# A two-layer graph network on one core: one segment sum as a 64-column matmul, another message order, and a rearranged prologue

## The chip, the core and the metric

The kernel runs on one core of a Trainium2 chip. The core has engines with queues of their own: TensorE (PE, with PEld for its weight loads), VectorE (DVE), ScalarE (ACT), GpSimd (POOL) and SyncE (SP); transfers are issued from a queue and run on 16 DMA engines. The metric is device time in microseconds (us). Everything is fp32. Seven runs of the kernel before took 5893.01 to 5935.96 us, with a median of 5921.59.

## The reference, cut to what matters

There are 6250 nodes with 160 features (64 scalars and 32 vectors of 3 components), and 200000 edges, sorted by destination. Each of two layers does this, and then adds x and normalizes:

```python
xs, xv  = mixed node features          # 64 scalars, 32 x 3 vector components
w       = silu(e @ W_fc1) @ W_fc2      # per edge: w0 (64), w1 (64), w2 (32), w3 (32)
gs, gv  = xs[src], xv[src]             # gathered by edge
mid0a   = w0 * gs * e_s                # "A": scalars from scalars
mid0b   = w3 * sum_c(gv * e_v) / sqrt3 # "D": scalars from vectors
mid1a   = w1 * gs * e_v                # "C": vectors from scalars
mid1b   = w2 * gv * e_s                # "B": vectors from vectors
agg     = segment_sum([mid0a, mid0b, mid1a, mid1b], dst) / 4
x       = layernorm(x + C_S * self(x) + C_X * mix(agg))
```

The second layer has 96 and 128 channels in place of some of these, and a gate at its end.

## The kernel before, in words

**Edges.** The 200000 edges are cut into 1563 tiles of 128. `plan()` (L37) puts 3 to 12 consecutive tiles into each of 284 groups such that the destinations of a group should fit a window of W = 32 nodes. In the prologue the kernel checks that they do; if the flag says so (L991), it takes the fast path `windows()` (L594), first for layer 1 (i = 0), then for layer 2, and otherwise a slow general path, which does not run here.

**The loop of `windows()`** (L831) goes over 391 units of four tiles, as a software pipeline. For each unit it

- gathers the source rows of the unit four ahead (`gather`, POOL, one indirect DMA a tile, L710, eight pair buffers);
- makes the hidden layer of the unit three ahead (`hidden`: PE matmuls into `pair`, ACT Silu into `h`, L672 and L683);
- makes the edge weights of the unit two ahead (`weights`: 192 columns a tile into a `pw` bank), the selectors `sel` (`places`, DVE, L741: for each tile four blocks of 32 columns, one each for e_s, e_x, e_y, e_z, with the edge attribute where the destination matches) and the messages `mid` (`products`, DVE, L728: four instructions for two tiles in layer 1);
- turns the sums of groups that ended in the unit before (`turn`, L775: PE transposes of `r` into the upper half of a `pair` bank, L143, then two DVE adds into `sm` and `sr`, L788 and L790, at a column offset loaded from `base`);
- sums its own four tiles (`aggregate`, L751);
- does one or two steps of the node blocks (`prepare` and `proceed`: tiles `pn`, `nx`, `xt`, `rm0`, `rr0`).

The order of PE instructions is pinned to program order (L138 and L143, the helpers `matmul` and `transpose`), so on PE a late operand holds up all that follows. Since all matmuls go through L138, its groups in a profile are told apart by their tiles and shapes.

**The sum.** In `aggregate` each selector block of a tile is a matmul of its own with 32 weight columns, at `tile_position=(0, 32 * c)`, so that the four results lie in the partitions 0, 32, 64 and 96 of one `pg` bank. Which of the 32-wide blocks of `mid` each multiplies is in `sums` (L605), as (first block, step, number):

```python
        sums = (((5, 2, 5), (0, 2, 3), (2, 1, 3), (2, 2, 3)),
                ((9, 1, 5), (2, 1, 5), (0, 2, 5), (0, 1, 5)))[i]
```

In layer 1 the selector of e_s therefore moves 160 columns and the other three 96 each. At a group's end ACT copies `pg` into `r` (L766: 128x96; L768: the other 64 columns of 32 rows).

**The prologue** (L148 to L430) takes the nodes in 13 chunks (twelve of four blocks of 128, then a tail of 106 rows). `turn_nodes` transposes a chunk on PE; the copies `xt` go to DVE and ACT in turn, and `zt` to ACT. `send_nodes` multiplies by `l1` and `l1z`, scales on ACT (L284), adds on DVE (L285) and stores to `table`. `check()` comes after the sixth chunk: two casts, a small matmul, 11 subtracts, three reduces and two subtracts on DVE, with `limits` set by POOL earlier. `checked()` makes the flag after the last chunk. Then 12 matmuls compose the weights of the node step (`w23` into a `pw` bank), and 13 small DVE copies put them into `rm0` and `rr0` (L389 to L397). The first gather on POOL (L710) comes after that.

Of the kernel before, what the change touches and what calls it, by code (L numbers as in the profile page):

```python
# [9 lines left out]
F32 = mybir.dt.float32  # L10
I32 = mybir.dt.int32
AF = mybir.ActivationFunctionType
OP = mybir.AluOpType
# [3 lines left out]
P = 128  # L17
# [69 lines left out]
def kernel(ctx: ExitStack, tc: tile.TileContext, a, out):  # L87
# [34 lines left out]
    SLOTS = (448, 640)  # L122
# [25 lines left out]
    chunks = [range(b, min(b + BG, NB - 1)) for b in range(0, NB - 1, BG)] + [range(NB - 1, NB)]  # L148
# [12 lines left out]
    def spread(t, s, v, n, q):  # L161

        nc.vector.memset(t, 0.0)
        q.dma_start(t[0:S, 0:n], a[s])
        for k in range(2):
            q.dma_start(t[S + k * V:S + k * V + V, n + k * V:n + k * V + V], a[v])
# [3 lines left out]
    spread(l1[:, 0], "Ws_l1_a", "Wv_l1_a", S, nc.scalar)  # L170
    spread(l1[:, 1], "Ws_l1_c", "Wv_l1_c", S, nc.scalar)
    ident = const.tile([P, P], F32, name="ident")
    make_identity(nc, ident)
    for j, (k, q) in enumerate((("a", nc.scalar), ("c", nc.gpsimd))):
        for r in range(0, P, V):
            q.dma_start(l1z[r:r + V, j, :], a[f"Wv_l1_{k}"])
# [47 lines left out]
    rm0 = const.tile([96, 4, 2, S + V], F32, name="rm0")  # L224
    rr0 = const.tile([64, 2, 2 * V], F32, name="rr0")
# [4 lines left out]

    limits = pre.tile([1, 2, NG], F32, name="limits")
    nc.gpsimd.memset(limits[:, 0], 0.0)
    for b, g in enumerate(READY):
        if g < NG:
            nc.gpsimd.memset(limits[:, 0, g:min(READY[b + 1], NG)], float(P * (b + 1)))
    g0 = 0
    while g0 < NG:
        g1 = g0
        while g1 < NG and zeroed(g1) == zeroed(g0):
            g1 += 1  # L240
        nc.gpsimd.memset(limits[:, 1, g0:g1], float(zeroed(g0) - W))
        g0 = g1

# [4 lines left out]
    def turn_nodes(bs, x):  # L248

        m, n = len(bs), rows_of(bs[0])  # L250
        p = psum.tile([P, 512], F32, name="pw", bufs=3)
        for j in range(m):
            transpose(p[:, j * P:j * P + n], x[:n, j, 0:P], ident[:n, :n])
        last = work.tile([P, BG * V], F32, name="xz")
        nc.vector.tensor_copy(last[:n, :m * V].rearrange("p (j d) -> p j d", d=V), x[:n, 0:m, P:D])
        z = pair[0][:, 0:P]
        transpose(z[:m * V, :n], last[:n, :m * V], ident[:n, :n])
        xt = work.tile([P, BG * P], F32, name="xt", bufs=2)
        zt = work.tile([P, P], F32, name="zt", bufs=2)
        w = (m - 1) * P + n  # L260
        if (bs[0] // BG) % 2:
            nc.scalar.activation(xt[:, :w], p[:, :w], AF.Copy)
        else:
            nc.vector.tensor_copy(xt[:, :w], p[:, :w])
        nc.scalar.activation(zt[:m * V, :n], z[:m * V, :n], AF.Copy)
        return xt, zt

    def send_nodes(bs, xt, zt):
        n = rows_of(bs[0])
        rows = work.tile([P, BG, D], F32, name="rg", bufs=2)  # L270
        qs = []
        for j in range(len(bs)):
            tag, k = (("pg", 2), ("pn", 1), ("pg", 2), (None, 0))[j]
            p = psum.tile([P, 512], F32, name=tag, bufs=k) if tag else pair[1]
            q = p[:n, :2 * D].rearrange("p (w d) -> p w d", w=2)
            matmul(q[:, :, 0:P], xt[:, j * P:j * P + n], l1, start=True, stop=True)
            qs.append(q)
        for j, q in enumerate(qs):
            v = slice(j * V, j * V + V)
            matmul(q[:, :, P:D], zt[v, :n], l1z[v], start=True, stop=True,  # L280
                   tile_position=(j * V, 0))
        for j, (b, q) in enumerate(zip(bs, qs)):
            t = rows[:n, j, :]
            nc.scalar.activation(t, q[:, 0, :], AF.Copy, scale=nv[:n, b, 0:1])  # L284
            nc.vector.scalar_tensor_tensor(t, q[:, 1, :], nv[:n, b, 1:2], t,  # L285
                                           op0=OP.mult, op1=OP.add)
        if n == P:
            nc.sync.dma_start(
                table[0][bs[0] * P:(bs[-1] + 1) * P, :].rearrange("(j p) d -> p j d", p=P),
                rows[:, :len(bs), :])  # L290
        else:
            nc.sync.dma_start(table[0][bs[0] * P:N, :], rows[:n, 0, :])
# [8 lines left out]

    def check():

        basef = pre.tile([1, NG], F32, name="basef")
        nc.vector.tensor_copy(basef, base)
        nc.vector.tensor_copy(off, raw)
        p = psum.tile([P, 512], F32, name="pw", bufs=3)
        matmul(p[:, :NG], ones, basef, start=True, stop=True)
        for g0, g1 in segments:
# [3 lines left out]
            nc.vector.tensor_tensor(o, o, p[:, g0:g1, None].to_broadcast([P, m, n]), OP.subtract)  # L313

        nc.vector.memset(off[tail_e:, NT - 1:], 0.0)
        ends = pre.tile([P, 2], F32, name="ends")
        nc.vector.tensor_reduce(ends[:, 0:1], off, AX.X, OP.max)
        nc.vector.tensor_reduce(ends[:, 1:2], off, AX.X, OP.min)

        nc.vector.tensor_scalar(ends[:, 0:1], ends[:, 0:1], float(W - 1), None, op0=OP.subtract)  # L320
        nc.vector.scalar_tensor_tensor(over, ends[:, 1:2], -1.0, ends[:, 0:1],
                                       op0=OP.mult, op1=OP.max)

        nc.vector.tensor_tensor(limits[:, 0], limits[:, 0], basef, OP.subtract)
        nc.vector.tensor_tensor(limits[:, 1], basef, limits[:, 1], OP.subtract)
        nc.vector.tensor_reduce(tops[:, 1:2], limits, AX.XY, OP.max)

    def checked():
# [7 lines left out]
    previous = None  # L336
    for c, (bs, x) in enumerate(zip(chunks, xs)):
# [4 lines left out]
        if c == 5:  # L342
            check()
    send_nodes(previous[0], *previous[1])
    checked()


# [26 lines left out]

    p = psum.tile([P, 512], F32, name="pw", bufs=3)
    q = p[:96, :192].rearrange("p (j d) -> p j d", j=2)

    for j in range(2):
        for o, w, m in ((q[:, j, 0:S], w23[:, j * 96:j * 96 + 96], w23[:, 192:256]),
                        (q[:, j, S:], w23[:, 256 + j * 96:352 + j * 96], w23[:, 448:480])):
            matmul(o, w, m, start=True, stop=True)
        for k in range(2):
            matmul(p[k * V:k * V + V, 192 + j * V:224 + j * V],
                   w23[:, 320 + j * 96:352 + j * 96], w23[:, 448:480], start=True, stop=True,
                   tile_position=(0, k * V))
    nc.vector.tensor_copy(rm0[0:64, 0, :, 0:S], q[0:64, :, 0:S])  # L389
    nc.vector.tensor_copy(rm0[64:96, 0, :, S:], q[64:96, :, S:])  # L390

    for c, at_c, at_d in ((1, (32, 64), 0), (2, (0, 64), 32), (3, (0, 32), 64)):
        for k, r in enumerate(at_c):
            nc.vector.tensor_copy(rm0[r:r + 32, c, :, S:], q[32 * k:32 * k + 32, :, S:])
        nc.vector.tensor_copy(rm0[at_d:at_d + 32, c, :, 0:S], q[64:96, :, 0:S])
    for k in range(2):
        nc.vector.tensor_copy(  # L397
            rr0[k * V:k * V + V, :, k * V:k * V + V],
            p[k * V:k * V + V, 192:256].rearrange("p (j d) -> p j d", j=2))
# [76 lines left out]
    def second_nodes(b, work, clear, name="nx"):  # L476
# [26 lines left out]
        def summed():  # L503
            p = psum.tile([P, 512], F32, name=bank[0], bufs=bank[1])
            q = p[:n, :2 * D].rearrange("p (w d) -> p w d", w=2)
            for c in range(4):
                l = sm[:96, c, rows]
# [6 lines left out]
            matmul(q[:, :, S + V:D], sr[:64, rows], rr0, start=False, stop=True)  # L514
# [79 lines left out]
    def windows(i, loads, work, inputs_of):  # L594
# [4 lines left out]
        scalar = lambda w, place: (w, V, 0, 2, place, 2)  # L599
        vector = lambda w, place, step, c=0, n=3: (w, 0, S + c * V, n, place, step)  # L600
        kinds = ((scalar(0, 2), scalar(S, 5), vector(128, 9, 2), vector(160, 0, 3)),
# [3 lines left out]
        sums = (((5, 2, 5), (0, 2, 3), (2, 1, 3), (2, 2, 3)),  # L605
                ((9, 1, 5), (2, 1, 5), (0, 2, 5), (0, 1, 5)))[i]
# [144 lines left out]
        def aggregate(t):  # L751
# [6 lines left out]
            for c, (at, step, k) in enumerate(sums):  # L758
                o = mid[:n, t % 2, V * at:V * at + V]
                o = bass.AP(tensor=o.tensor, offset=o.offset, ap=[o.ap[0], [V * step, k], [1, V]])  # L760
                matmul(pg[32 * c:32 * c + 32, :k * V], s[:n, t % 2, c, :], o,
                       start=first, stop=last, tile_position=(0, 32 * c))
            if last:
                r = work.tile([P, 160], F32, name="r")
                w = (96, P)[i]
                nc.scalar.activation(r[:, :w], pg[:, :w], AF.Copy)  # L766
                if i == 0:
                    nc.scalar.activation(r[:32, 96:], pg[:32, 96:160], AF.Copy)  # L768
# [6 lines left out]
        def turn(g):  # L775
            r = made["r", g]
            pt = pair[g % 2][:, 2 * P:]
            if i == 0:
                transpose(pt[:96, :P], r[:, :96], ident)
                transpose(pt[:64, P:P + W], r[:32, 96:160], ident[:32, :32])  # L780
            else:
                transpose(pt[:, :P], r[:, :P], ident)
                matmul(pt[:, P:P + W], rest[g % 3], fold, start=True, stop=True)
            with tc.issue_after(made["last"].ins):
                b = nc.vector.value_load(base[0:1, g:g + 1], min_val=0, max_val=NP - W)  # L785
            at = bass.ds(b, W)
            h, k = ((96, 64), (P, P))[i]
            nc.vector.tensor_tensor(  # L788
                sm[:h, :, at], pt[:h, :P].rearrange("p (c w) -> p c w", c=4), sm[:h, :, at], OP.add)
# [90 lines left out]
    def general(i, loads, work):  # L880
# [18 lines left out]
        def body(t, n):  # L899
# [51 lines left out]
            if i == 0:  # L951
                put = [a0, a1, bx, dx, c0[1], c1[1], c0[2], dy, c1[2], c0[3], c1[3], dz, by, bz]
# [25 lines left out]
        h = (96, P)[i]  # L978
        into = [(h * k, h, lambda c, k=k: sm[:h, k, c]) for k in range(4)]
        into.append((4 * h, slots - 4 * h, lambda c: sr[:slots - 4 * h, c]))  # L980
# [76 lines left out]
```

## Time and profile before

| | value |
|---|---|
| median of 7 runs | 5921.59 us (5893.01 to 5935.96) |
| the profiled execution: time, span | 5933.25 us, 5931.5 us |
| mean granted TensorE clock | 0.75 |
| busy PE / PEld / DVE / ACT / POOL | 4430.0 / 2879.7 / 3052.3 / 1172.3 / 3078.7 us |
| first gather | 65.64 us after the start |

The table is of the profiled execution but for its first line. Busy time is a union of an engine's instructions, and matmuls overlap, so a mean duration times a count is more than the busy time. The duration of a single matmul includes its way through the array: what one costs in a row of many is read from the starts. A matmul in fp32 appears as two records, its two passes. In a line "a <-b", b is what ended the idle time of a. Layer 1 lies between some 66 and 3000 us, layer 2 after it.

### The profile page before, as it was taken

To read this page: it belongs to the slowest core of one execution; us is meant where nothing else is said; L and a number is where in the kernel's file an instruction comes from. 1 tells how busy PE (TensorE), PEld (TensorE's weight loads), DVE (VectorE), ACT (ScalarE), POOL (GpSimd) and SP (SyncE) were. 2 spreads that over 40 slices of the span, in tenths; PEclk is the share of its full clock that TensorE was granted. 3 is DMA by queue.
4 is the path that set the end of the run, shared out by engine and by line. 5 is a ranking of instruction groups with operands and counts; after the bars stand their busy time and mean duration, and the time that the engine had idled before them with its cause. 6 is when DMAs were issued, how large, how long until landed. Compare 5 with 4: busy or idle time off the path is not lost. (4 is left out here: it accounts for less than half of the span.)

```text
span 5931.5 us, 108061 instructions
## 1 busy us (share of the span) xinstructions
PE 4430.0 (75%) x37363; PEld 2879.7 (49%) x37363; DVE 3052.3 (51%) x13202; ACT 1172.3 (20%) x4012; POOL 3078.7 (52%) x3232
## 2 busy tenths in 40 slices
PE   7788777777777777787866676777677776777877
PEld 4555555555555555555534444444444444444544
DVE  5554444444444454444545555555555555555555
ACT  2111111111122222222210111111112222222333
POOL 4555555555555455454445555555555555544543
PEclk7777777777777777777777777777777777777777
DMA  3222222222222222222222222222222222222221
GB/s 102 60 61 59 57 56 55 53 55 52 55 54 54 50 56 55 52 55 52 53 63 66 66 69 68 71 67 68 66 67 67 68 69 67 65 63 64 66 64 44
DMA packets 298517, 364.06 MB, mean 61 GB/s; under 512 B 86323, under 2 KB 246204, under 8 KB 297964
## 3 DMA queue, kind: packets, MB, share of 16 engines
q0 software_dynamic: 151056, 257.36, 18.0%
q1 hardware_dynamic: 121740, 85.59, 5.6%
q10 hardware_dynamic: 25168, 14.11, 0.8%
q8 instruction: 301, 4.93, 0.3%
q14 instruction: 252, 2.06, 0.1%
HBM read 338.73 MB, written 18.03 MB: 60 GB/s over the span
## 5 line engine op out<-in xcount | busy, mean ns | idle before, releaser
L710 POOL DMA_INDIRECT g<-table,src x3126 | 3056.9, 978 | 2811.3 <-DVE mid L728 1579.6
L728 DVE TENSOR_TENSOR mid<-g,pw 128x128 f32<-128x128 f32 (+2 forms) x7820 | 1840.8, 297 | 426.8 <-remote 197.2
L138 PE MATMUL pg<-mid,sel 128*32 128x160 f32 (+1 forms) x25008 | 1582.3, 353 | 245.1 <-issue 242.9
L138 PE MATMUL pw<-fc,h 100*128 100x192 f32 (+1 forms) x6252 | 1491.7, 432 | 289.4 <-issue 229.9
L138 PEld LDWEIGHTS pw<-fc,h 100*128 100x128 f32 (+1 forms) x6252 | 1051.0, 233 | 778.6 <-issue 705.8
L741 DVE SCALAR_TENSOR_TENSOR sel<-iota,off,ea 128x128 f32<-128x128 f32 x3126 | 945.8, 340 | 686.0 <-remote 412.5
L138 PEld LDWEIGHTS pg<-mid,sel 128*32 128x32 f32 x25008 | 945.4, 133 | 629.3 <-issue 489.5
L143 PE MATMUL pair<-ident,r 128*96 128x128 f32 (+1 forms) x852 | 264.2, 335 | 704.1 <-ACT h L683 314.5
L138 PE MATMUL pair<-e,fc 64*100 64x256 f32 (+1 forms) x2348 | 727.7, 524 | 75.7 <-issue 49.6
L788 DVE TENSOR_TENSOR sm<-pair,sm 96x128 f32 (+1 forms) x568 | 163.9, 289 | 1177.1 <-PE pair L143 357.6
L143 PEld LDWEIGHTS pair<-ident,r 128*96 128x96 f32 (+1 forms) x852 | 125.1, 147 | 927.5 <-ACT h L683 356.8
L766 ACT ACTIVATE r<-pg 128x96 f32<-128x96 f32 (+1 forms) x568 | 149.7, 264 | 1977.0 <-remote 866.7
L138 PEld LDWEIGHTS pair<-e,fc 64*100 64x100 f32 (+1 forms) x2348 | 300.6, 215 | 322.0 <-issue 266.7
L672 ACT ACTIVATE h<-pair 100x256 f32<-100x256 f32 x782 | 258.3, 378 | 925.3 <-remote 357.2
L683 ACT ACTIVATE h<-pair 128x256 f32<-128x256 f32 x392 | 150.3, 384 | 957.7 <-remote 380.4
L138 PE MATMUL pn<-rm,sm 96*128 96x128 f32 (+3 forms) x968 | 199.7, 353 | 50.6 <-issue 42.0
L138 PEld LDWEIGHTS pn<-rm,sm 96*128 96x128 f32 (+2 forms) x968 | 177.5, 235 | 71.8 <-issue 61.5
L772 ACT ACTIVATE rest<-pg 32x32 f32<-32x32 f32 x1136 | 209.5, 184 | 12.8 <-issue 0.3
L517 DVE SCALAR_TENSOR_TENSOR nx<-pn,gets,nx 128x160 f32<-128x160 f32 x96 | 36.5, 380 | 200.1 <-PE pw L138 71.4
L138 PEld LDWEIGHTS pair<-fold,rest 128*128 128x128 f32 x568 | 132.8, 285 | 13.5 <-ACT rest L772 8.1
L458 ACT ACT_TABLE_LOAD x95 | 121.9, 1283 | 1.9 <-DVE mv L457 0.3
L143 PE MATMUL pn<-ident,nx 128*128 128x128 f32 (+1 forms) x242 | 65.4, 362 | 74.0 <-DVE nx L460 67.9
(153 smaller groups left out, 1473.5 us busy)
## 6 DMA issues: line engine op xcount, KB each, us to landing
g<-table,src POOLq DMA_INDIRECT x3126
e<-in_e SPq DMA_DIRECT2D x781, 64.0 KB
e<-in_e SPq DMA_DIRECT2D x390, 20.0 KB
ea<-in_ea_main SPq DMA_DIRECT2D x63, 96.0 KB
xg<-in_x_main SPq DMA_DIRECT2D x12, 320.0 KB
table<-rg SPq DMA_DIRECT2D x12, 320.0 KB
xmid<-nx ACTq DMA_DIRECT2D x48, 80.0 KB
table<-nr ACTq DMA_DIRECT2D x48, 80.0 KB
```

The source lines that it names most:

```text
L138: r = nc.tensor.matmul(*args, **kw)
L143: r = nc.tensor.transpose(*args)
L458: nc.scalar.activation(mv[:n, 1:2], mv[:n, 1:2], AF.Sqrt, bias=eps[:n])
L517: nc.vector.scalar_tensor_tensor(y, q[:, k, :], gets[:n, b, k:k + 1], y, op0=OP.mult, op1=OP.add)
L672: nc.scalar.activation(h[:100, 2 * P * j:2 * P * j + m], pair[j][:100, :m], AF.Silu)
L683: nc.scalar.activation(h[:kk, c0:c1], p[:kk, c0:c1], AF.Silu, scale=0.125)
L710: nc.gpsimd.indirect_dma_start(out=g[:n, j, :], out_offset=None, in_=table[i][:, :], in_offset=bass.IndirectOffsetOnAxis(ap=of(t)[0], axis=0))
L728: nc.vector.tensor_tensor(parts(mid[:n, :m], V * place, V * step, k), parts(g[:n, :m], c, V, k), parts(q[:n, :m], w, w_step, k), OP.mult)
L741: made["last"] = nc.vector.scalar_tensor_tensor(s[:n, j], iota[:n, None, :].to_broadcast([n, 4, W]), w, e[:, :, None].to_broadcast([n, 4, ...
L766: nc.scalar.activation(r[:, :w], pg[:, :w], AF.Copy)
L772: nc.scalar.activation(rest[g % 3][k, k], pg[k, P:P + V], AF.Copy)
L788: nc.vector.tensor_tensor(sm[:h, :, at], pt[:h, :P].rearrange("p (c w) -> p c w", c=4), sm[:h, :, at], OP.add)
```

## The change

The y and z selector blocks of layer 1 become one matmul with 64 weight columns. For that both must multiply the same blocks of `mid`, so the order of messages in layer 1 becomes Dx, C0, Dy, C1, Dz, A0, A1, Bx, By, Bz. e_s takes the five last (160 columns), e_x the first four, and e_y and e_z both the blocks 1 to 4 (128 columns; what one of them doesn't need is computed too and multiplied by zero weights later, or meets its own weights in `rm0`):

```diff
-        sums = (((5, 2, 5), (0, 2, 3), (2, 1, 3), (2, 2, 3)),
-                ((9, 1, 5), (2, 1, 5), (0, 2, 5), (0, 1, 5)))[i]
+        sums = (((0, 1, 5, 1, 5), (1, 1, 0, 1, 4), (2, 2, 1, 1, 4)),
+                ((0, 1, 9, 1, 5), (1, 1, 2, 1, 5), (2, 1, 0, 2, 5), (3, 1, 0, 1, 5)))[i]
...
-            for c, (at, step, k) in enumerate(sums):
+            for c, m, at, step, k in sums:
...
-                matmul(pg[32 * c:32 * c + 32, :k * V], s[:n, t % 2, c, :], o,
+                matmul(pg[32 * c:32 * (c + m), :k * V],
+                       s[:n, t % 2, c:c + m, :].rearrange("p c w -> p (c w)"), o,
                        start=first, stop=last, tile_position=(0, 32 * c))
             if last:
                 r = work.tile([P, 160], F32, name="r")
-                w = (96, P)[i]
-                nc.scalar.activation(r[:, :w], pg[:, :w], AF.Copy)
+                nc.scalar.activation(r[:, :P], pg[:, :P], AF.Copy)
                 if i == 0:
-                    nc.scalar.activation(r[:32, 96:], pg[:32, 96:160], AF.Copy)
+                    nc.scalar.activation(r[:32, P:], pg[:32, P:P + V], AF.Copy)
```

A tile of layer 1 thus has three matmuls: 32 weight columns with 160 moved, 32 with 128, and 64 with 128, in this order. Layer 2's matmuls are those of before. What hangs on it: `sm` takes 128 rows in layer 1 (96 before) and `sr` 32 (64), the turn transposes 128 and 32 columns, `rm0` and `rr0` are laid out accordingly, and a node block has one matmul more:

```diff
-            matmul(q[:, :, S + V:D], sr[:64, rows], rr0, start=False, stop=True)
+            matmul(q[:, :, S + V:S + 2 * V], sm[:, 0, rows], rr0[:, 0], start=False, stop=False)
+            matmul(q[:, :, S + 2 * V:D], sr[:V, rows], rr0[:V, 1], start=False, stop=True)
```

The prologue is arranged anew: the tail chunk comes first; `l1` is cleared once; of the loads of `l1` and `l1z`, ACT issues the four of "a" and POOL the four of "c" (before, ACT issued ten and POOL four); the `xt` copy of the tail goes to DVE; the casts, the 11 subtracts, the clearing of `limits` and its two subtracts move to POOL; the reduces stay on DVE, one a chunk, after the last add of that chunk; the weights are composed after the eighth chunk, copied by ACT out of PSUM, and placed by DVE in steps of three a chunk; the flag is made ahead of the last `send_nodes`:

```diff
-    chunks = [range(b, min(b + BG, NB - 1)) for b in range(0, NB - 1, BG)] + [range(NB - 1, NB)]
+    chunks = [range(NB - 1, NB)] + [range(b, min(b + BG, NB - 1)) for b in range(0, NB - 1, BG)]
...
-            nc.vector.tensor_tensor(o, o, p[:, g0:g1, None].to_broadcast([P, m, n]), OP.subtract)
+            nc.gpsimd.tensor_tensor(o, o, base_of[:, g0:g1, None].to_broadcast([P, m, n]),
+                                    OP.subtract)
...
-        if c == 5:
+        if c == 3:
+            nc.gpsimd.tensor_copy(basef, base)
+            nc.gpsimd.tensor_copy(off, raw)
+        if c == 6:
+            bases()
             check()
+        if c == 7:
+            small = composed()
+        if c > 7:
+            for step in small[:3]:
+                step()
+            small = small[3:]
+        if c > 8 and reduces:
+            with tc.issue_after(last[0].ins):
+                reduces.pop(0)()
+    assert not small and not reduces
+    checked()
     send_nodes(previous[0], *previous[1])
-    checked()
```

## The prediction, before the result was known

> **What bounds the kernel now.** I read the busy shares first, then layer 1 alone (100 to 2950 us): its windows, its waits and its TensorE groups with the shapes kept apart, then timelines of single units, and last the prologue. The window of layer 1 (columns: length, then busy time and instructions of PE, PEld, DVE, ACT and POOL, granted clock, DMA share, GB/s), and what PE waited for there (total, times, longest):
>
> ```profile
> 100.00:2950.00 2850.00, 2231.56 (x18717) 1509.52 (x18709) 1379.04 (x5712) 532.38 (x1698) 1510.39 (x1539) 0.75 0.23 55
> ```
> ```profile
> PE pair L143 <- ACT h L672: 281.7, 85, 7.5
> PE pg L138 <- issue: 100.0, 179, 1.2
> PE pn L143 <- DVE nx L460: 64.6, 38, 7.3
> ```
>
> PE is busy 2232 of 2850 us; no other engine passes 1511. The 618 us of idle PE are few and long (the first line: 85 waits of 3.3 us). A layer has 391 units of four tiles, so one takes about 7.3 us, 5.7 of them PE work; POOL's four gathers take 4 x (0.98 + 0.30) = 5.1 us. So layer 1 is a PE chain with holes, at a granted clock of 0.75 (slices of 2 us show 1.00 and 0.50, with 0.50 after a hole).
>
> Next the groups that the change touches (busy, mean ns; then idle before), and two stretches of PE (start, length, instructions), the first two lines at clock 1.0, one unit at 0.5, then two tiles at each clock:
>
> ```profile
> L138 PE MATMUL pw<-fc,h 100*128 100x192 f32 x3080 | 803.7, 409 | 52.3 <-issue 49.1 <-DVE mid L728 1.1 <-PE pair L138 0.3
> L138 PE MATMUL pg<-mid,sel 128*32 128x160 f32 x3082 | 710.2, 380 | 17.1 <-issue 16.6
> L138 PE MATMUL pg<-mid,sel 128*32 128x96 f32 x9247 | 549.8, 307 | 84.1 <-issue 83.4
> ```
> ```profile
> 1015.22 1.57 PE L138 MATMUL pw<-fc,h 100*128 100x192 f32 x8
> 1016.71 1.27 PE L138 MATMUL pg<-mid,sel 128*32 128x160 f32 x32
> ```
> ```profile
> 1005.02 2.34 PE L138 MATMUL pg<-mid,sel 128*32 128x160 f32 x32
> ```
> ```profile
> 1028.98 1.28 PE L138 MATMUL pg<-mid,sel 128*32 128x160 f32 x16
> ...
> 1032.80 0.73 PE L138 MATMUL pg<-mid,sel 128*32 128x160 f32 x16
> ```
>
> A unit's sum is 4 tiles x 4 matmuls x 2 passes of fp32 = 32 records. At clock 1.0, 32 take 1.27 us and 16 take 0.73, so two tiles more cost 0.54: **0.27 us a tile**; at 0.5, (2.34 - 1.28) / 2 = **0.53 us**. The eight pw records of 192 columns take 1.57 us, and a row of five 1.08: 0.163 us each, 0.85 ns a column. Two passes of 160 columns are thus 0.27 us, while a tile's four matmuls one after another would be 2 x (160 + 3 x 96) x 0.85 = 0.76. So the four column strips run beside each other, and only the widest, 160 columns, is paid for.
>
> **The change, part by part.**
>
> *Fewer matmuls in a tile's sum.* 4 become 3, or 8 records fewer of some 98 in a unit. But the x strip keeps its 160 columns. If the 64-column matmul still runs beside the other two, a tile costs 0.27 us as before: nothing gained. The three narrow strips ended early and hid behind the wide one; at 128 columns they still do.
>
> *A second tile shape.* This is the price I expect to decide. In the trace, PE waits whenever the shape of its array tile changes. From the last pw (100 x 128) to the first pg (128 x 32), from pg to pair, and from pair to pw, the next matmul starts 93 to 97 ns after the stream before it could have ended at clock 1.0, and 134 to 138 ns at 0.5 (medians over hundreds of pairs); between matmuls of one shape it is 2 ns. The wait is also there where the tiles don't overlap: after the 32-row whoz matmuls, none of 91 pair matmuls on rows 64 to 127 starts within 200 ns, though those rows are free; after a 64-row tile on rows 0 to 63 they start 13 ns later. So two shapes don't share the array. No row shows 128 x 32 beside 128 x 64, so the cost has two ends: nothing, if these two can mix; or, if not, per tile a group of two 32-column strips (2 x 160 columns), a switch, the 64-column group (2 x 128 columns, alone), and a switch back. The Trainium skill, "TensorEngine Tiling (Array Packing)", section Tiling Modes, speaks against the change: it lists 128x64 and 128x32 as separate configurations and says "Changing tiling mode (not just tile) drains the TensorE"; it gives no duration; by it the sum takes the upper end, without it nothing.
>
> The upper end: a 64-column group is 128/160 of 0.27 or 0.53, so 0.21 or 0.43 us. Four tiles add 4 such groups and 7 switches (the first into pg and the last out of it are there now):
> clock 1.0: 4 x 0.213 + 7 x 0.095 = 1.52 us a unit; clock 0.5: 4 x 0.427 + 7 x 0.137 = 2.67 us.
> At a mean clock of 0.75 half the time, so two thirds of the work, is at 1.0: 2/3 x 1.52 + 1/3 x 2.67 = 1.90 us. Times 391: **743 us** of PE time. I take this end, since the nearest rows (switches in columns from 128 to 32, in rows between disjoint tiles) all drain.
>
> How much of it reaches the end? PE's holes can take some. The turn (L143) waits for the r copy and ACT h, 281.7 us, and node steps for DVE nx, 64.6 us: together 346, in which PE has nothing else in its fixed order; a later pg would fill them only if what it waits for does not itself come after pg. ACT's r copy does come after pg, so 346 is generous; all 618 us of idle PE is the other bound. So +743 - 346 = **+397 us**, between +125 (743 - 618) and +743. Late next would be POOL: at 5.1 of then 8.3 us a unit it is further off than now, so no cover from there.
>
> *mid in another order, r, sm and the turn.* The same four DVE products a pair, of the same sizes. r goes from 128x96 and 32x64 to 128x128 and 32x32; ACT is busy 532 of 2850 us. The first transpose has 128 weight columns for 96, with the same 128 moved. sm adds 128 rows for 96, sr 32 for 64: DVE lengths go by elements per row, which stay. One more matmul per node block: 49 x 2 passes x 64 columns x 0.85 ns = 5 us at most, halved clocks aside; taken in the range, 0 here.
>
> *Prologue.* The first gather starts at 65.64, held by the small copies into rr:
>
> ```profile
> POOL g L710 <- DVE rr L397: 39.7, 1, 39.7
> ```
> ```profile
> 7.23 1.28 ACT L265 ACT_TABLE_LOAD   x1 [7.23 <-DMA l<-in_Wv_l_c]
> ```
> ```profile
> 30.03 2.41 DVE L313 TENSOR_TENSOR off<-off,pw 128x444 f32<-128x444 f32 x11
> ...
> 33.32 1.76 DVE L317 TENSOR_REDUCE ends<-off 128x1 f32<-128x1563 f32 x1
> 35.01 1.76 DVE L318 TENSOR_REDUCE ends<-off 128x1 f32<-128x1563 f32 x1
> ...
> 37.48 0.67 DVE L264 COPY xt<-pw 128x512 f32<-128x512 f32 x1
> ```
>
> Three savings. ACT issues ten loads before its table load, about 0.5 us each (its queue rows 0.76 to 7.20); six fewer let it start about 3 us sooner, though the first x must be there too: -3 to 0. Check holds DVE from 30.03 to 37.48, and PE has a hole of 6.07 us before 38.49. The subtracts and casts (2.41 + 0.87 + 1.02 us) go to POOL, which stands idle for 39.7 us; the reduces (2 x 1.76 + 0.72) stay on DVE, spread over three chunks behind the last rg. I take 4 of the hole's 6 us. POOL's price for a subtract is not shown; from its 128x768 memset (0.76 us) to its 128x128 ident (0.33 us), 1563 columns of cast and subtract are 3 to 8 us, and with the limits' memsets (0.33 + 0.71 + 2.42) still inside the cover; without cover a late check would hold the last reduce and the first gather by what it lacks, a few us. The 13 copies into rm0 and rr0 (61.83 to 65.1, 3.3 us) are spread over chunks where DVE waits for ACT; the flag and the last send remain: -2.5. The queues: on SP the short tail of x goes first; POOL issues four l1 loads as before (others than before), ahead of its dst loads. Sum **-10 us**, from 0 to -13.
>
> **Sum.** The profiled run took 5933.25 us (span 5931.5), 12 above the median of 5921.59. 5933 + 397 - 10 = **6320 us**.
>
> **Rivals.**
>
> *A: the shapes mix.* The 64-column matmul runs beside the others. For: both use all 128 rows, and the strips run independently now. Against: every other switch seen. Then only the prologue counts: 5933 - 10 = 5923, no change to be told.
>
> *B: faster, since fewer matmuls shorten the holes.* In the trace, pg's last matmul often counts as finished 0.7 to 8 us late while three or more gathers run back to back; the turn then waits (281.7 us <-ACT h), the clock falls to 0.5, and the next unit runs at half speed. I can't explain these holes. If they come from the number of pg matmuls in flight (a quarter fewer now), they shrink: about 98 in layer 1 are over 2.5 us, 517 us in sum; a quarter is 130, so 5933 - 10 - 130 = 5793. It needs A too, or a gain above the drain's price. It decides against me from 397 us of holes closed.
>
> *C: the full price.* The added PE time makes pg, r and the turn later in every unit, no hole fills, and 0.5-clock stretches last longer: 5933 + 743 - 10 = 6666. For it: by a fit over layer 1's units, a microsecond of node matmuls goes with 2.4 (± 0.3) us more of its unit, so PE time is hardly ever hidden.
>
> *D: the holes take all.* 5933 + 125 - 10 = 6048.
>
> **Chances.** Forecast with its neighbours C and D: drain, 0.75 (forecast 0.45, C 0.17, D 0.13). A 0.12, of which 0.07 within 0.3% and 0.05 faster; B 0.13. A difference under 0.3% (18 us) can't be told from none here. So faster 0.18, same 0.07, slower 0.75. The range leaves out the ends of B and C: 5780 to 6700.
>
> **What would show it.** In layer 1, pg stretches of a unit with 24 records of 2.8 us at clock 1.0 instead of 32 of 1.27, 64-column records starting 95 ns after the 32-column stream, PE busy in the layer up by some 700 us, the ACT h wait shrunk. If pg still takes 1.27, A or B holds, and the number and length of the <-ACT h waits tells which. In the prologue, the first gather near 56. I would be wrong if two column widths share the array, or if the holes go with the matmuls' number.

## The result, and the profile after

The changed kernel takes **6005.58 us** (median of 19 runs, 5936.12 to 6056.32) against 5925.79 us for the kernel before (46 runs, 5888.35 to 5962.09): the ratio is 1.0118, with a 95% interval of 1.010 to 1.0137. It is slower, as forecast, but by 80 us between the medians (70 by the ratio) and not by the 387 of the prediction. The ratio leaves out runs over 1.5% above the fastest, the profiled execution (6030.64 us, span 6028.9) among them; its clock, 0.796, is that of the others (0.793 to 0.812).

Layer 1 in the same window as before (length, then busy time and instructions of PE, PEld, DVE, ACT and POOL, granted clock, DMA share, GB/s), and three lines of what PE waited for there:

```profile
100.00:2950.00 2850.00, 2600.92 (x15277) 1466.79 (x15275) 1338.75 (x5546) 514.05 (x1633) 1490.43 (x1501) 0.84 0.22 53
```
```profile
PE pair L143 <- ACT h L701: 168.9, 68, 6.1
PE pn L143 <- DVE nx L487: 15.6, 13, 3.4
PE pg L138 <- issue: 14.9, 33, 0.9
```

PE is busy for 2601 us of the window instead of 2232, at a granted clock of 0.84 instead of 0.75. The waits that the prediction listed are shorter: 169 us for 282, 16 for 65, and 15 for 100. The groups that the change touches:

```profile
L138 PE MATMUL pg<-mid,sel 128*32 128x160 f32 x3000 | 798.7, 353 | 4.2 <-issue 4.2
L138 PE MATMUL pg<-mid,sel 128*64 128x128 f32 x2998 | 745.3, 335 | 8.2 <-issue 7.9
L138 PE MATMUL pg<-mid,sel 128*32 128x128 f32 x3000 | 699.2, 320 | 3.1 <-issue 2.9
L138 PE MATMUL pw<-fc,h 100*128 100x192 f32 x3000 | 684.2, 378 | 3.0 <-issue 2.9
```

The 64-column matmuls are busy for 745 us. The three pg groups overlap, so this line does not yet say that they don't hide behind the others; the starts below do. The pw matmuls, which nobody changed, take 684 us instead of 804 for nearly as many: the higher clock. One unit of the changed kernel at clock 1.0:

```profile
522.16 3.08 PE L138 MATMUL pg<-mid,sel 128*32 128x160 f32 x24
525.16 0.68 PE L138 MATMUL pair<-e,fc 64*100 64x256 f32 x4
```

From the first of the 24 records to the next operation it takes 3.00 us. In the kernel before, 32 records took 1.21, from 1016.71 in the prediction's stretch to the next operation:

```profile
1017.92 0.46 PE L138 MATMUL pair<-e,fc 64*100 64x256 f32 x2
```

The medians over the whole units of layer 1 are 3.01 and 1.20 us at clock 1.0, and 5.16 and 2.27 at 0.5. Between a 32-column and a 64-column matmul, in either direction, the next starts 95 to 96 ns (at clock 1.0) after the stream before it could have ended, as at the switches of shape in the prediction (93 to 97 ns).

To see where the layer's time went, I give each moment from the first gather to the last of layer 1 either to the matmul that PE is in (of two that overlap, the later) or to idle:

| layer 1, us | pg | pw, pair, pn | idle | sum | clock |
|---|---|---|---|---|---|
| before | 726 | 1519 | 637 | 2882 | 0.750 |
| after | 1373 | 1308 | 271 | 2952 | 0.843 |
| difference | +647 | -211 | -366 | +70 | |

So 647 us were added. Idle time took 366 of them, and 211 came back because all other matmuls ran at the higher clock: if each moment of pw, pair and pn is weighted with the granted clock, they take 1131 us before and 1114 after, so their work hardly changed. The 70 us that are left are most of the 97 between the two profiled spans. The rest lies outside layer 1: layer 2, whose instructions are the same, took 2919 us for 2906, and the passage between the layers 53 for 39.

In the prologue nothing was won between these two executions. The first gather starts at 65.68 us (65.64 before):

```profile
58.80 3.65 SPq L279 DMA_DIRECT2D table<-rg  x2
```
```profile
65.68 1.05 POOL L739 DMA_INDIRECT g<-table,src  x1 [23.12 <-issue]
```

The last store of `table` is issued at 62.05 (the second of the two) and its semaphore reaches POOL at 64.53; in the kernel before it was issued at 61.52 and came at 64.33. The gather follows 1.2 to 1.3 us later in both. Single executions scatter here: over all traces of the experiments below and these two, the first gather comes at 65.6 to 67.4 us in the four executions that have the prologue of before (before, before_too, slow_before, yz_only; mean 66.6), and at 61.3 to 66.4 in the eight with the whole new one (mean 64.0). So some 2 to 3 us are won on average, of the 10 that were forecast.

### The profile page after: what moved, and what is told of

The parts are those of the page before. It is cut to its first block, busy times and chain, and to the rows that moved or that the text cites. A ratio compares the mean times of both kernels' runs of the same rounds, so it can differ in the third digit from the quotient of the medians.

```text
span 6028.9 us, 101994 instructions
## 1 busy us (share of the span) xinstructions
PE 4887.0 (81%) x34331; PEld 2876.6 (48%) x34331; DVE 3049.4 (51%) x13185; ACT 1176.2 (20%) x4015; POOL 3117.0 (52%) x3248
## 5 line engine op out<-in xcount | busy, mean ns | idle before, releaser
L138 PE MATMUL pg<-mid,sel 128*32 128x160 f32 x21882 | 2268.4, 361 | 190.4 <-issue 188.6
L138 PEld LDWEIGHTS pg<-mid,sel 128*32 128x32 f32 x21882 | 1057.6, 132 | 1203.0 <-issue 1106.3
L138 PE MATMUL pw<-fc,h 100*128 100x192 f32 (+1 forms) x6252 | 1367.0, 417 | 200.5 <-issue 148.8
L816 DVE TENSOR_TENSOR sm<-pair,sm 128x128 f32 x568 | 165.3, 291 | 1357.5 <-PE pair L143 531.6
L143 PE MATMUL pair<-ident,r 128*128 128x128 f32 x852 | 245.0, 313 | 610.9 <-ACT h L712 352.1
L795 ACT ACTIVATE r<-pg 128x128 f32<-128x128 f32 x568 | 157.2, 277 | 1945.2 <-PE pg L138 999.0
L143 PEld LDWEIGHTS pair<-ident,r 128*128 128x128 f32 x852 | 118.9, 140 | 813.7 <-ACT h L712 395.6
L138 PE MATMUL pn<-rm,sm 128*128 128x128 f32 (+3 forms) x968 | 180.1, 333 | 17.8 <-issue 17.1
L138 PEld LDWEIGHTS pn<-rm,sm 128*128 128x128 f32 (+1 forms) x968 | 161.8, 218 | 28.7 <-issue 26.4
L138 PE MATMUL pair<-fold,rest 128*128 128x32 f32 x568 | 112.1, 285 | 8.7 <-issue 5.5
```

The costliest lines, as they stand in the source:

```text
L138: r = nc.tensor.matmul(*args, **kw)
L143: r = nc.tensor.transpose(*args)
L795: nc.scalar.activation(r[:, :P], pg[:, :P], AF.Copy)
L816: nc.vector.tensor_tensor(sm[:, :, at], pt[:, :P].rearrange("p (c w) -> p c w", c=4), sm[:, :, at], OP.add)
```

## The experiments

My theory after the result: two widths of column tile don't share the array, as forecast, but what of that time is paid is what idle PE and the granted clock don't take, and the prologue is worth nothing, since the last store of `table` is the gate. The rivals: the loss comes from the rest of the layer's change (message order, 128 rows of `sm`, the matmul more in a node block), or from the prologue, or switching does harm beyond its TensorE time.

The experiments ran in five groups, each on one chip, and each is compared with the kernel before on its chip. That matters here: in four groups the kernel before takes 4097 to 4103 us instead of 5926. Only one group (tail_first, early_mix, late_check, slow_bal) met a chip like the first, with 5834.

### One part alone

Layer 1 as before, with the new prologue (`p_only`). 

> Layer 1 as before, the prologue of the change alone. Theory: the prologue is worth nothing, since the first gather waits for the last table store to land (64.33 us before, 64.53 after), so the first gather stays at 65.5 to 66 us and the ratio is 1.000 (0.998 to 1.002). Rival, the step on record: first gather near 56 us, 10 us less, ratio 0.998. Second rival: the prologue carries part of the loss, ratio 1.003 or more.

Measured: 4129.44 against 4103.35 us, ratio 1.0076 (1.0047 to 1.0106). The first gather is at 61.6 us (67.4 in the kernel before on that chip). Neither my theory nor the forecast holds: the prologue makes the kernel slower. This is taken up below.

The prologue as before, with the change in layer 1 (`yz_only`). 

> Prologue as before, the layer-1 sums and message order of the change alone. Theory: the whole loss is here, ratio 1.010 to 1.014, clock in layer 1 0.84 for 0.75, TensorE idle in layer 1 down by some 360 us. Rival (prologue carries part of it): 1.007 or less.

Measured: 4439.58 us, ratio **1.0832** (1.0808 to 1.0855), clock 0.996 in layer 1, 39 us idle. The loss is in layer 1, but it is 336 us here, nearly five times the result's. All that I had expected of its size was wrong, which made the chip itself the question.

```diff
-        sums = (((0, 1, 5, 1, 5), (1, 1, 0, 1, 4), (2, 2, 1, 1, 4)),
+        sums = (((0, 1, 5, 1, 5), (1, 1, 0, 1, 4), (2, 1, 1, 1, 4), (3, 1, 1, 1, 4)),
```

That edit makes y and z two matmuls of 32 weight columns again, with all else as changed (`split`). 

> The changed kernel with y and z as two matmuls of 32 weight columns and 128 moved each, all else as changed. Theory (the 64-column shape is the cause): a unit's sum takes 1.27 us at clock 1.0 again, layer 1's clock is back at 0.75, ratio 0.998 to 1.002. Rival (message order, 128-row sm, the matmul more in a node block): the loss stays, 1.010 to 1.014.

```profile
536.24 1.27 PE L138 MATMUL pg<-mid,sel 128*32 128x160 f32 x32
537.45 0.49 PE L138 MATMUL pn<-who,xt 128*128 128x128 f32 x2
```

Measured: 1.0058 (1.0039 to 1.0077); the unit's sum is 1.21 us again, and layer 1 takes 2027 us with 268 idle at a clock of 0.906 (the kernel before on this chip: 2016, 262 and 0.902). The loss in layer 1 is gone, so the message order, the 128-column strips and the additional node matmul cost next to nothing. What is left is that of `p_only`.

The changed kernel with a unit's 32-column matmuls ahead of its 64-column ones (`quad`):

```diff
-                for t in range(4 * u, min(4 * u + 4, NT)):
-                    if t == 4 * u + 2:
-                        prepare()
-                    aggregate(t)
...
+                for t in ts:
+                    aggregate(t, (0, 1) if i == 0 else range(4), i == 1)
+                if i == 0:
+                    if len(ts) > 2:
+                        prepare()
+                    for t in ts:
+                        aggregate(t, (2, 3))
```

> The changed kernel with all 32-column matmuls of a unit first and its four 64-column matmuls after them: one switch of shape inside a unit instead of seven, the same streams. Theory (a 64-column group runs alone and is paid in full, and switches come on top): the unit's sum at clock 1.0 takes 1.27 + 4 x 0.21 + 0.1 = 2.2 us instead of 2.8, so two thirds of the loss are left, ratio 1.006 to 1.010. Rival (only the switches cost, the 64-column streams are hidden): 1.5 us, ratio 1.000 to 1.003.

```profile
532.43 2.29 PE L138 MATMUL pg<-mid,sel 128*32 128x160 f32 x24
534.65 0.49 PE L138 MATMUL pn<-who,xt 128*128 128x128 f32 x2
```

Measured: 2.22 us from the first record to the next operation, so both the streams and the switches are paid, as the theory has it. The ratio is 1.0178 (1.0156 to 1.020), above the expected range, which was meant for the first chip: 39 us more in layer 1 than the kernel before has there, where the change costs 325.

### The chip, and what TensorE time is

The kernel before (`before_too`) and the changed one (`after_too`) once more on the chip of the first group. 

> The kernel before once more, for its profile on the chip on which the others run. Where it takes about 4100 us, theory: TensorE idle in layer 1 of 250 to 300 us instead of 635, few holes over 2.5 us, granted clock above 0.9, first gather at 65.5 to 66.5 us. Rival (the shorter time comes from faster gathers or vector work): POOL and DVE instructions are shorter than on the first chip (978 and 297 ns), clock and holes as there.

> The changed kernel once more. A unit's sum costs 3.0 us at clock 1.0 for 1.2, so 1.8 x 391 = 708 us. Theory: holes and clock pay for a part of it, so on a chip with 270 us of idle TensorE in layer 1 the rest is +300 to +400 us, ratio 1.075 to 1.095; on a chip with 635 us of idle 1.010 to 1.014 again. Rival (a loss that does not go with the chip's holes): 1.012 everywhere.

The windows of both, from 100 to 2000 us, before and then after:

```profile
100.00:2000.00 1900.00, 1649.26 (x17774) 1170.84 (x17772) 1309.95 (x5417) 504.58 (x1594) 1429.84 (x1479) 0.90 0.32 79
```
```profile
100.00:2000.00 1900.00, 1878.46 (x12947) 1093.17 (x12944) 1127.23 (x4661) 416.71 (x1320) 1276.99 (x1291) 0.99 0.27 68
```

Measured: 1.0883 (1.0853 to 1.0912) for `after_too`. Gathers and vector instructions are no shorter on this chip (median gather 946 ns, 949 on the first). What differs is PE's holes. On the first chip, ACT's copy of a finished `pg` into `r` often starts late although ACT is free. Of the copies in layer 1 before which ACT already stood idle when the last pg matmul ended, these start over 0.7 us after that end:

| run | late copies | in sum |
|---|---|---|
| before (first chip) | 88 of 252 | 412 us |
| after (first chip) | 30 of 261 | 131 us |
| before_too | 0 of 261 | 0 |
| after_too | 0 of 274 | 0 |
| yz_only | 0 of 275 | 0 |

In 81 of the 88, three or more gathers ran back to back (less than 0.4 us apart) between the matmul's end and the copy. In before_too, 209 of the 261 copies fall into such rows of gathers, and none is late. Layer 1 by the same division of time:

| layer 1, us | pg | pw, pair, pn | idle | sum | clock |
|---|---|---|---|---|---|
| before_too | 529 | 1225 | 262 | 2016 | 0.902 |
| after_too | 1168 | 1135 | 38 | 2341 | 0.986 |
| filler | 1182 | 1125 | 20 | 2326 | 0.996 |
| quad | 862 | 1128 | 66 | 2055 | 0.991 |

The change adds 639 us to pg here, as many as on the first chip (647). But there were only 262 us of idle time to fill, of which 224 went, and little clock to gain, which gave back 90, so 325 are paid.

The changed kernel without a second shape but with as much TensorE time (`filler`), by y and z apart and

```diff
+                if (i, c) == (0, 0):
+                    o = mid[:n, t % 2, 0:272]
+                    matmul(pg[:32, 160:432], s[:n, t % 2, 0, :], o,
+                           start=False, stop=last, tile_position=(0, 0))
```

> The changed kernel with y and z as two matmuls of 32 weight columns, and 272 columns more moved on the first strip of every tile (their sums are used by nothing): no second shape, but about the TensorE time of the changed kernel, 2 x 432 x 0.833 = 0.72 us a tile, 3.0 us a unit at clock 1.0. Theory (the loss is TensorE time, whatever it is spent on): the same time as the changed kernel on the same chip, within 1%. Rival (switching itself stalls other engines or the handing on of results): at least 2% faster than the changed kernel.

```profile
533.37 3.11 PE L138 MATMUL pg<-mid,sel 128*32 128x160 f32 x40
536.41 0.68 PE L138 MATMUL pair<-e,fc 64*100 64x256 f32 x4
```

Measured: 1.0833 (1.0811 to 1.0855), 4438.9 us against 4456.41. The same time within 0.4%. The switches harm by the TensorE time they take and by nothing else that this can show.

### Idle time made on purpose

If idle time and clock absorb the change, then idle time made on a chip without holes must do it too. Three memsets ahead of every gather of layer 1 make POOL the bound (`slow_before`, and `slow_after` with the change):

```diff
+                    for _ in range(3 * (i == 0)):
+                        nc.gpsimd.memset(g[:n, j, :], 0.0)
                     nc.gpsimd.indirect_dma_start(
```

> The kernel before, with three memsets of the target tile ahead of every gather of layer 1, on POOL: 3 x 0.25 us (between 0.17 for 128x100 and 0.28 for 128x192) on 1.26 us, so layer 1 is bound by POOL at some 2.0 us a gather, 3100 us, and TensorE idles for over 1000 us of it at a lower granted clock. It is the base for slow_after.

> The changed kernel with the same memsets. Theory (what idle TensorE and its clock can't take is what the change costs): with over 1000 us idle nearly all of the 708 us is absorbed; 0 to 60 us more than slow_before. Rival (the 64-column shape costs its 1.8 us a unit wherever it stands): 250 us more or over.

Measured: 5041.4 and 5077.66 us, 36 us or 0.7% apart. PE idles for 660 us of slow_before's layer 1, not for the 1000 that I had expected. Layer 1, 100 to 3000 us, before and then after:

```profile
100.00:3000.00 2900.00, 2251.72 (x18562) 1541.86 (x18561) 1403.92 (x5671) 537.89 (x1686) 2320.86 (x6121) 0.74 0.22 54
```
```profile
100.00:3000.00 2900.00, 2617.34 (x15516) 1483.89 (x15512) 1393.67 (x5635) 530.20 (x1674) 2320.64 (x6089) 0.85 0.21 53
```

These are nearly the numbers of the first chip: PE busy 2252 to 2617 us, the clock from 0.74 to 0.85. By the division of time, pg takes 656 us more, the other matmuls 268 less, idle time 372 less, which leaves some 15 (layer 2 with its longer gathers, taken up below, adds 14). With idle time from another source the same change costs almost nothing: what is shown is that idle time and clock take it, not what makes the holes of the first chip.

### Four even strips

If only the widest strip is paid for, it can be made narrower without another shape (`bal`, from the kernel before): e_s moves four blocks, its fifth (Bz) goes under the x strip in a small matmul, and y and z move four. Then `r` is 128x128, with one transpose and one vector add a turn.

```diff
-        sums = (((5, 2, 5), (0, 2, 3), (2, 1, 3), (2, 2, 3)),
+        sums = (((5, 2, 4), (0, 2, 3), (2, 1, 4), (0, 2, 4)),
...
+                if (i, c) == (0, 1):
+                    matmul(pg[V:2 * V, 3 * V:P], s[:n, t % 2, 0, :], mid[:n, t % 2, 13 * V:14 * V],
+                           start=False, stop=last, tile_position=(0, V))
```

> The kernel before with four even strips in layer 1: e_s moves A0, A1, Bx, By (128 columns), a small matmul more puts e_s times Bz under the x strip (32 columns beside its 96), y and z move 128; one transpose and one vector add a turn instead of two. Theory (the widest strip is all that is paid, shapes unchanged): 1.20 - 8 x 32 x 0.833 ns = 0.99 us a unit's sum at clock 1.0, and 0.2 us less a turn: 82 + 57 us of TensorE time less, of which holes and a falling clock take half: ratio 0.975 to 0.99 on a chip with few holes, 0.99 to 1.0 on one with many. Rival (a strip's three weight loads a tile show): 1.2 us a unit or more, only the turn's gain is left, 0.99 to 1.005.

```profile
554.69 1.13 PE L138 MATMUL pg<-mid,sel 128*32 128x128 f32 x40
555.75 0.68 PE L138 MATMUL pair<-e,fc 64*100 64x256 f32 x4
```

Measured: **0.9928** (0.9911 to 0.9944), 4069.4 us: faster than both kernels on that chip. The unit's sum is 1.06 us, between the expected 0.99 and the 1.20 of before. The gain is smaller than the expected 0.975 to 0.99. Of 57 us less in pg and 43 less in pair, some 21 are left in layer 1's 1994 us: idle time grew by 39, and pw and pn by 39 together, pw because the clock fell from 0.902 to 0.890, pn also by its additional matmuls. The same feedback, the other way. How much of the gain is the narrower strip and how much the turn with one transpose and one add less, this run can't tell. 

> The four even strips once more. On a chip with few holes the theory expects 0.991 to 0.995 as measured; on a chip where TensorE idles for some 600 us in layer 1, less TensorE time is worth little: 0.994 to 1.003. Rival (the gain is not TensorE time but the vector add and the copy less a turn): 0.993 on either.

`bal_again`: 0.9938 (0.9921 to 0.9954), again on a chip with few holes. 

> The four even strips, with the three memsets ahead of every gather of layer 1. Theory: where TensorE idles for 660 us, less TensorE time is worth little: within 15 us of slow_before (5041 us), ratio of the two 0.997 to 1.000. Rival (the gain seen, 0.7%, is not TensorE time): 30 us or more less.

`slow_bal` came to a chip with holes, where the kernel before takes 5834 us, so it can't be set against slow_before (another chip): 5978.07 us, some 780 us idle in layer 1. It decides nothing. Whether the even strips gain on a chip like the first stays open.

> The changed kernel with y and z as two matmuls of 32 weight columns, once more. On a chip with few holes 1.004 to 1.008 as measured (the longer gathers). On a chip with 600 us of idle TensorE, theory (the 64-column shape is the cause there too): layer 1's clock at 0.75 to 0.77, idle near 610 us, ratio 0.998 to 1.005. Rival (there it is another part of the layer's change): 1.010 or more.

`split_again`: 1.0085 (1.0062 to 1.0109), on a chip with few holes. That the 64-column shape is the cause on the first chip too is therefore argued from its trace (drains, pg's 647 us), not shown by a run there.

### The prologue

All kernels with the new prologue have longer gathers. Layer 2 of `before_too` and of `p_only`, 2130 to 4050 us:

```profile
L710 POOL DMA_INDIRECT g<-table,src x1529 | 1455.6, 952 | 465.8 <-issue 386.0 <-DMA g<-table,src 22.3 <-DVE mid L728 21.0
```
```profile
L737 POOL DMA_INDIRECT g<-table,src x1516 | 1458.6, 962 | 461.9 <-issue 390.0 <-DVE mid L755 23.2 <-DMA g<-table,src 18.3
```

With few holes, layer 2 is a chain of gathers: 1563 x (0.952 + 0.305) = 1965 us, and it takes 1963. So 10 ns a gather are 16 us, and layer 2 takes 1979 in `p_only`. Over both layers, 11 ns (the medians are 946 and 957) times 3126 are 34 us at most, and the first gather comes some 6 us earlier: that can account for the loss of p_only (26) and split (23). On the first chip the medians are 949 and 957. The instructions of the layers are the same in order and kind in `p_only` as in the kernel before.

Five runs took the new prologue apart, each from the kernel before. Its loads alone: 

> The kernel before with only the loads of l1 and l1z of the change (ACT four, POOL four, one of them spread over 128 partitions by a zero stride). The kernels with the new prologue have a median gather of 957 ns for 946, 3126 of them. If these loads cause it: 957 ns, and ratio 1.004 to 1.009. If not: 946 ns, ratio 0.998 to 1.001.

Its POOL instructions alone: 

> The kernel before with only the casts, the 11 subtracts and the two of limits on POOL. If POOL's vector instructions ahead of the gathers cause the longer gathers: median 957 ns, ratio 1.004 to 1.009. If not: 946 ns, ratio 0.998 to 1.001.

The order of chunks alone: 

> The kernel before with only the order of the chunks changed: the short tail first. Kernels with the whole new prologue have a median gather of 957 ns for 946; neither the loads nor POOL's vector instructions caused it. If the order of the chunks does (first rows of table written, DMA queue and semaphore of each store): 957 ns and ratio 1.004 to 1.009. If not: 946 ns, ratio 0.998 to 1.002, first gather within 1 us of 66.

The early weights alone: 

> The kernel before with only the composed weights made early, copied by ACT and placed in steps of three. If this causes the longer gathers: 957 ns and ratio 1.004 to 1.009. If not: 946 ns; the first gather then tells what the 13 copies at the end cost: by the step on record 2.5 us less, by the theory that the last store of table is the gate under 1 us less.

The order of the check alone: 

> The kernel before with the reduces one a chunk, the memsets of limits late and the flag ahead of the last send, all subtracts still on DVE. If this causes the longer gathers: 957 ns, ratio 1.004 to 1.009. If not: 946 ns. If none of the three has 957 ns, the cause is in their sum, such as the number of instructions or the place of the program, and stays open.

| run | ratio | median gather | last store issued, first gather |
|---|---|---|---|
| pool_loads | 1.0011 (0.9988 to 1.0033) | 946 ns | 61.53, 65.5 us |
| pool_check | 1.0025 (1.0003 to 1.0046) | 946 ns | 66.66, 70.8 us |
| tail_first | 1.0018 (1.0001 to 1.0035) | 946 ns | 67.21, 71.0 us |
| early_mix | 1.0006 (0.9991 to 1.0021) | 949 ns | 63.40, 67.5 us |
| late_check | 0.9983 (0.9957 to 1.0009) | 946 ns | 58.18, 62.3 us |

No part has 957 ns, so the cause of the longer gathers is not found; it lies in the sum of the parts or in what they share, and stays open. (Where a chip has holes, the gathers don't bound the kernel, so for the last three it is the median that tells, not the ratio.) The last column answers the other question: in all five the first gather comes 3.8 to 4.1 us after the last store of `table` is issued, also where the small copies into `rr0` are gone from the end (`early_mix`). For `tail_first` I had expected it within 1 us of 66; it came at 71.0, with the store.

## Why the prediction was wrong

It had the sign, the place and the drain right, and missed the size by a factor of about five. By its own steps:

**The drain: right, somewhat too small.** The row that I chose (switches drain even between disjoint tiles) holds: 95 to 96 ns at clock 1.0. The unit's sum at 1.0 is 3.0 us, forecast 2.8. In the trace the second pass of a 64-column matmul starts 53 ns after its first could have ended, and that of the 128-column x strip 26 ns; I had counted 2 ns between matmuls of one shape. At the old clock the measured units would have made it (2/3 x 1.80 + 1/3 x 2.89) x 391 = some 845 us instead of 743. The rule of the Trainium skill, "TensorEngine Tiling (Array Packing)", section Tiling Modes, that I cited agrees with the trace.

**The holes: the sum right, by luck.** I took 346 us of idle time as filled; it was 366. But I had taken it from two waits, and in the window these fell by only 162 us (282 to 169 for ACT h, 65 to 16 for DVE nx). Most of the rest came from many short waits that the view gives as "issue" and that I had not counted: 235 us before, 46 after.

**The step that failed: "At a mean clock of 0.75 half the time".** I priced the added work at the clock of before, and all other work of PE as if its durations stood still. But the clock rose with PE's load: with fewer holes it was 0.843. The pg time grew by 647 us and not by the 845 of the old clock, and pw, pair and pn, which the change hardly touches, took 211 less. The clock was thus worth some 410 us for which the sum has no term: 743 - 346 = 397 had to be 845 - 366 - 410 = some 70. The trace's clock records hold 1.00 and 0.50 and nothing between, and the share of 1.00 in layer 1 rose from 0.50 to 0.69. This agrees with the Trainium skill, "TensorE: Matmul & The Clock Gate", Part 1, which says that activity releases the throttle. The rows that told it stood in my own prediction (0.50 after a hole): filling holes also speeds up what comes after them.

**The price at its full, rival C (+743), and A.** Where PE has few holes, 325 us of 639 are paid, so C's "no hole fills" holds in no run here. A (no drain) is refuted by the 64-column rows. D's 6048 lies nearest the result, but not by its mechanism: not all 618 us of idle time were filled, and the clock did the rest.

**Rival B** (fewer matmuls shorten the holes): its forecast, a faster kernel, is refuted. Its mechanism is neither shown nor refuted. On the first chip the late copies of `r` fell from 88 (412 us) to 30 (131 us), and the idle stretches of PE over 2.5 us from 69 (316 us in sum; the prediction's 98 and 517 us are too many for these) to 47. That may be because PE was busy in their place, or because there were fewer pg matmuls. `slow_before` and `slow_after`, on a chip without late copies, show that filling alone can take as much (372 us); no run changes the number of matmuls alone on a chip with late copies.

**The prologue: wrong.** Of the three savings, none reached the first gather in the two executions on the first chip, and 2 to 3 us on average over all traces. The 2.5 us of copies stood beside the landing of the last store (64.33 us), which let the gather begin no earlier; I took the releaser that the view named for the only one. PE's hole of 6 us went, but the last add of the last full chunk started at 61.65 instead of 59.91, for the first chunk's started 2.9 us later (17.27 for 14.37, the tail ahead of it), and a reduce ahead of the `xz` copy of a late chunk made a new one:

```profile
53.05 0.30 PE L143 MATMUL pair<-ident,xz 128*128 128x128 f32 x1 [2.23 <-DVE ends L336]
```

That the prologue could make the gathers longer (957 ns for 946) was in none of the cases.

## What to carry to other kernels

Price added TensorE time in three terms, not two: the work, the idle time it fills, and the clock that the filled idle time brings to all other matmuls; here the last gave back 211 us of 647. The same sum read backwards says that less TensorE time gains less than its length, where the clock falls with it: with the four even strips, 100 us less in pg and pair left some 21. And a loss that idle time hides is a loss still: on a chip without the holes this change costs 8.8% instead of 1.2%.

## What the runs showed that I had not expected

- The same kernel takes 4100 us on some chips and 5830 to 5930 on others, with the same instructions of the same length. On the slow ones, ACT's copy of a finished `pg` starts over 0.7 us late while gathers run back to back (88 of 252 copies against 0 of 261). Why is not known.
- The prologue, with identical instructions after it, changes a gather's time on POOL from 946 to 957 ns for the whole of both layers. None of the five parts that were tried does so alone.
- A strip can take a second matmul a tile for little: with 128 columns on each strip, one of them in two matmuls (96 and 32), a unit's sum fell from 1.20 to 1.06 us, where the expectation's estimate for the widest strip alone was 0.99.
